# Per-token head attention: the softmax quotient in two vector instructions instead of three

## The chip, the cores and the metric

The kernel runs on one core of a Trainium2 chip. Time is the device time of one execution in microseconds (us); the median of three runs is compared. The core has five engines that run side by side, each strictly in the order of its own queue: TensorE (PE, matrix products; PEld is its weight load), VectorE (DVE), ScalarE (ACT), GpSimd (POOL) and SyncE (SP, which starts transfers). They wait for each other through semaphores. Two memories lie on the core: SBUF[...] and PSUM, into which TensorE writes.

## The reference

The program has two layers: a depthwise convolution with routed experts, and then attention and a second routed network. The change concerns the attention. It is not over tokens but, for every token, over the 16 elements of each of 8 heads:

```python
attn = (q * scale)[..., :, None] * k[..., None, :]   # per token and head: 16 x 16
attn = softmax(attn, axis=-1)
out = einsum('bhlij,bhlj->bhli', attn, v)
```

So for each token, head h and query element i, the result is the sum over j of exp(q_i k_j) v_j, divided by the sum over j of exp(q_i k_j). The tokens are the pixels of 32 images of 56 x 56, 100,352 in all, with 128 channels each.

## The kernel before

The attention stage goes through the tokens in 784 tiles of 128 tokens. Seven tiles are a group, and there are 112 groups. Much of the work is done for two tiles, a pair, at a time, so there are 392 pairs. The steps of a tile or pair, by the function names of the code, with the tile names as the profile writes them:

- keys (TensorE, per pair): keys and values of two tiles into PSUM, kv.
- ends (VectorE, per pair, kx<-kv): the largest and smallest key of every head, two reductions.
- pivots (GpSimd, per pair, kx<-kx, c<-q,kx and c<-c,kx): the key that gives the largest product, c. Three instructions; a pair that crosses a group has one more.
- offsets (VectorE, per tile, s<-kv,c): key minus pivot for 16 x 128 pairs of elements, s.
- scores (GpSimd, per tile, s<-s,q): multiplied by the query, in place.
- exps (ScalarE, per tile, s<-s): the exponential, in place.
- values (VectorE, per tile, ev<-s,kv): exponential times value, ev.
- sums (TensorE, per tile, sm<-ident,s and sm<-ident,ev): the 16 slices of s and of ev are added up in PSUM by transposes that accumulate. The tile sm of a pair holds, for both tiles, the sums of exponentials and the sums of products: [128 channels, 2 tiles, 2 kinds, 128 tokens].
- inverse_first (ScalarE, per pair, r<-sm, r<-r): an approximate inverse r of the sums of exponentials, as exp(-ln(sum)).
- quotients (VectorE, per pair, sm<-sm,r, r<-sm,r and oT<-sm,r): a Newton step for the inverse and the product with it; this is what changes.

Around these lie the head of each group (loading its tokens, normalizing, queries) and its tail (projection, residual, gate logits), mostly on ScalarE and TensorE. A small step of the tail, root_step, has four instructions on GpSimd for every group (st<-st). After every seventh group a pair of images is complete, and choose picks the eight best tokens per expert. It has three long instructions on VectorE: fm<-lg, lg<-fm,lg and pb<-lg,pb, the last a combination of two SBUF tiles.

The order of the work is written out by hand. The wrapper InOrder keeps the order of the text on each of the four compute engines. One loop over k issues, at each turn, work of several tiles: quotients of pair k-6, offsets and scores of tile k, values of tile k-2, and so on; where ends, quotients and pivots go once in two turns, quotients come with an even k, ends and pivots with an odd one. The group_work of places 2k and 2k+1 is the heads, tails and choices; the first of them follows the offsets of its turn on VectorE and precedes the values. So the order on VectorE for a pair of turns is: quotients, offsets, values, ends, offsets, values; on GpSimd: scores, pivots, scores.

All these instructions go through the wrapper, so the profile shows line 161 for each, and they are told apart by their tiles.

Of the kernel before, what the change touches and what calls it, by code (L numbers as in the profile page):

```python
# [8 lines left out]
F32 = mybir.dt.float32  # L9
# [3 lines left out]
ALU = mybir.AluOpType  # L13
# [4 lines left out]
P = 128  # L18
# [7 lines left out]
def conv_attn_hybrid_kernel(  # L26
# [25 lines left out]
    N, C, H, W = x.shape  # L52
# [148 lines left out]
    with tc.tile_pool(name="cv_c", bufs=1) as cc, tc.tile_pool(  # L201
        name="cv", bufs=3
# [147 lines left out]
    with tc.tile_pool(name="rt_c", bufs=1) as cc, tc.tile_pool(  # L350
        name="rt", bufs=4
# [92 lines left out]
    with tc.tile_pool(name="sel", bufs=1) as se, tc.tile_pool(  # L444
        name="sel2", bufs=2
# [257 lines left out]
    with tc.tile_pool(name="sc_c", bufs=1) as cc, tc.tile_pool(  # L703
        name="sc", bufs=4
# [50 lines left out]
        pe, ve, ac = (InOrder(e) for e in (nc.tensor, nc.vector, nc.scalar))  # L755
# [102 lines left out]
    with tc.tile_pool(name="ex_w", bufs=2) as ew, tc.tile_pool(  # L858
        name="ex", bufs=3
# [126 lines left out]
    with tc.tile_pool(name="at_c", bufs=1) as cc, tc.tile_pool(  # L986
        name="at", bufs=2
# [55 lines left out]
        pe, ve, sc, gp = (InOrder(e) for e in (nc.tensor, nc.vector, nc.scalar, nc.gpsimd))  # L1043
# [68 lines left out]
        trs, zrs, roots, qs_, oTs, t2s, us, lgt = ({} for _ in range(8))  # L1112
# [86 lines left out]
        def quotients(n):  # L1199

            r, sm = rs.pop(n), sms.pop(n)
            d = sm[:, :, 0, :]
            ve.tensor_tensor(d, d, r, ALU.mult)
            ve.scalar_tensor_tensor(r, d, -2.0, r, ALU.add, ALU.mult)
            (g, j), (g1, j1) = divmod(n, GJ), divmod(n + 1, GJ)
            for x, y in ((g, j), (g1, j1)):
                if y == 0:
                    oTs[x] = at.tile([C, GJ, P], F32, name="oT")
            if g == g1:
                ve.tensor_tensor(oTs[g][:, j : j + 2, :], sm[:, :, 1, :], r, ALU.mult)  # L1210
            else:
                ve.tensor_tensor(oTs[g][:, j, :], sm[:, 0, 1, :], r[:, 0], ALU.mult)
                ve.tensor_tensor(oTs[g1][:, j1, :], sm[:, 1, 1, :], r[:, 1], ALU.mult)


        def load(g):
# [287 lines left out]
        while k < NT or work or choosing or choices:  # L1504
            tile_work(k, 5, inverse_first, 2)
            tile_work(k, -1, ends, 2)
            tile_work(k, 6, quotients, 2)
            tile_work(k, 0, offsets)
            tile_work(k, -1, pivots, 2)
            tile_work(k, 0, scores)  # L1510
            tile_work(k, -2, keys, 2)
            tile_work(k, 3, sums_ev)
            group_work(2 * k)
            tile_work(k, 1, exps)
            tile_work(k, 2, values)
            tile_work(k, 2, sums_s)
            group_work(2 * k + 1)
            if k == NT + 4:
                for i in range(3):
                    fetch(i)  # L1520
            k += 1
# [3 lines left out]
    with tc.tile_pool(name="f_c", bufs=1) as cc, tc.tile_pool(  # L1525
        name="f", bufs=2
    ) as fp, tc.tile_pool(name="f_p", bufs=1, space=PSUM) as fps, tc.tile_pool(
        name="o", bufs=2
# [114 lines left out]
```

## Time and profile before

| what | us |
|---|---|
| median of three runs | 9744.74 |
| lowest, highest | 9736.06, 9754.17 |
| profiled execution, its own time | 9744.63 |
| profiled execution, span from first to last instruction | 9742.9 |
| attention stage, first offsets to last values | 4733.6 to 9177.5 |
| mean granted TensorE clock, share of full | 0.927 |

| engine | busy us in the span | share |
|---|---|---|
| TensorE (PE) | 8445.6 | 87% |
| VectorE (DVE) | 6563.1 | 67% |
| ScalarE (ACT) | 5231.5 | 54% |
| GpSimd (POOL) | 7059.9 | 72% |

The profile is that of one execution. A row of the groups gives line, engine, operation, the tile written and the tiles read, shapes and count; then the busy time in us and the mean of one instruction in ns; then the time the engine was idle just ahead of these instructions and what ended most of it. A row of the timeline gives the start in us, the duration in us, and the same names. A row of a tile's view gives the count, the shortest, median and longest duration in ns, and the first and last start. A wait that an instruction makes inside its own execution is part of its duration. The shares of the table are means over stages with different limits, so the stage of the change has to be read by itself.

### The profile page before, as it was taken

The numbers are of one execution on the slowest core, as the hardware profiler recorded it, in microseconds if no ns is written. First come the engines' busy times: TensorE is split into PE (matmuls) and PEld (weight loads), VectorE is DVE, ScalarE is ACT, GpSimd is POOL, SyncE is SP. The second block draws the span as 40 slices with busy tenths as digits, with TensorE's granted clock in tenths as the row PEclk, the third lists the DMA queues.
The fourth block names the chain that finished last, engine by engine and source line by source line (L and its number), as shares of the span: only waits on it lengthen the run. The fifth ranks groups of instructions, "written<-read, shape, count | busy, mean of one in ns | idle before, by whom it ended". The sixth has DMA issues, their size and how long they took to land. (4 is left out here: it accounts for less than half of the span.)

```text
span 9742.9 us, 159125 instructions
## 1 busy us (share of the span) xinstructions
PE 8445.6 (87%) x59112; PEld 6817.5 (70%) x59112; DVE 6563.1 (67%) x11135; ACT 5231.5 (54%) x13401; POOL 7059.9 (72%) x5460
## 2 busy tenths in 40 slices
PE   8988255656599999999899999999999999999878
PEld 4446144444367666666689999999999999999833
DVE  3348765556422222222699999999999999999723
ACT  0028422222233333333588888888888888888600
POOL 2228155555578777777899999999999999999600
PEclk9999588888799999999999999999999999999855
DMA  9995055555444444444100100000000000000199
GB/s 180 193 180 173 0 157 148 149 143 150 127 75 61 70 71 69 68 69 68 32 24 31 34 31 31 31 31 31 24 31 34 31 31 31 31 31 24 64 311 333
DMA packets 981784, 828.60 MB, mean 85 GB/s; under 512 B 517844, under 2 KB 873495, under 8 KB 961522
## 3 DMA queue, kind: packets, MB, share of 16 engines
q1 hardware_dynamic: 459410, 473.36, 17.8%
q0 software_dynamic: 177664, 188.81, 11.2%
q10 hardware_dynamic: 343936, 156.26, 6.4%
q8 instruction: 468, 7.67, 0.3%
q14 instruction: 306, 2.51, 0.1%
HBM read 465.46 MB, written 353.64 MB: 84 GB/s over the span
## 5 line engine op out<-in xcount | busy, mean ns | idle before, releaser
L161 POOL TENSOR_TENSOR s<-s,q 128x2048 f32<-128x2048 f32 x784 | 3599.2, 4608 | 74.6 <-DVE s L161 65.9
L161 ACT ACTIVATE s<-s 128x2048 f32<-128x2048 f32 x784 | 1505.0, 1920 | 683.1 <-POOL s L161 680.7
L161 POOL DMA_INDIRECT t_d<-ys,xe x992 | 1530.6, 1543 | 405.7 <-issue 229.0
L161 DVE TENSOR_TENSOR s<-kv,c 128x2048 f32<-128x2048 f32 x784 | 1786.8, 2279 | 20.4 <-POOL c L161 20.4
L161 DVE TENSOR_TENSOR ev<-s,kv 128x2048 f32<-128x2048 f32 x784 | 1784.1, 2276 | 4.5 <-ACT s L161 4.1
L161 PE MATMUL sm<-ident,ev 128*128 128x128 f32 x12544 | 1535.7, 277 | 53.5 <-DVE ev L161 53.5
L161 PE MATMUL sm<-ident,s 128*128 128x128 f32 x12544 | 1512.1, 274 | 8.6 <-ACT s L161 8.5
L161 PEld LDWEIGHTS sm<-ident,ev 128*128 128x128 f32 x12544 | 1438.4, 144 | 104.2 <-DVE ev L161 61.8
L161 PEld LDWEIGHTS sm<-ident,s 128*128 128x128 f32 x12544 | 1391.0, 142 | 21.4 <-ACT s L161 9.4
L932 ACT ACTIVATE hT<-ph,b1t 128x512 f32<-128x512 f32 (+1 forms) x992 | 679.7, 685 | 1236.5 <-PE ph L928 1220.9
L741 POOL DMA_INDIRECT xb_d<-xs,rd x784 | 764.9, 976 | 662.4 <-DVE xs L161 437.2
L943 DVE TENSOR_TENSOR ys<-py,b2t 128x512 f32<-128x512 f32 (+1 forms) x248 | 171.4, 691 | 1541.6 <-PE py L938 1269.3
L938 PEld LDWEIGHTS py<-w,hT 128*128 128x128 f32 x7936 | 958.1, 192 | 201.9 <-issue 91.9
L938 PE MATMUL py<-w,hT 128*128 128x128 f32 x7936 | 982.3, 277 | 0.2
L928 PE MATMUL ph<-xeT,w 128*128 128x512 f32 (+1 forms) x1984 | 921.7, 597 | 69.5 <-DVE xeT L924 69.5
L161 PE MATMUL pa<-rw,ct 128*128 128x256 f32 x1568 | 478.7, 455 | 559.7 <-DVE xs L161 489.4
L161 PEld LDWEIGHTS pa<-rw,ct 128*128 128x128 f32 x1568 | 341.8, 229 | 704.9 <-DVE xs L161 517.4
L161 DVE SCALAR_TENSOR_TENSOR xs<-pa,rst,add 128x256 f32<-128x256 f32 x784 | 351.7, 481 | 544.0 <-remote 432.6
L161 ACT COPY add<-px 128x512 f32<-128x512 f32 x224 | 119.0, 532 | 1043.9 <-remote 671.6
L928 PEld LDWEIGHTS ph<-xeT,w 128*128 128x128 f32 x1984 | 348.6, 191 | 391.8 <-issue 293.3
L240 PE MATMUL cps<-xin,br 56*64 56x448 f32 (+1 forms) x3584 | 452.0, 586 | 52.7 <-ACT ea L273 37.9
L161 PE MATMUL kv<-wq,zT 128*128 128x256 f32 x1568 | 419.4, 391 | 58.6 <-DVE ev L161 58.3
(564 smaller groups left out, 13351.7 us busy)
## 6 DMA issues: line engine op xcount, KB each, us to landing
ct<-conv_d SPq DMA_DIRECT2D x192, 448.0 KB
xin<-in_x_dram SPq DMA_DIRECT2D x128, 392.0 KB
conv_d<-ot ACTq DMA_DIRECT2D x256, 196.0 KB
t_d<-xs ACTq DMA_DIRECT2D x112, 448.0 KB
tr<-t_d SPq DMA_DIRECT2D x112, 448.0 KB
to<-t_d SPq DMA_DIRECT2D x32, 1568.0 KB
out_dram<-oo ACTq DMA_DIRECT2D x32, 1568.0 KB
xg<-in_x_dram SPq DMA_DIRECT2D x96, 448.0 KB
```

What stands on the lines that cost most here:

```text
L161: r = getattr(self.engine, name)(*a, **k)
L240: nc.tensor.matmul(pss[r][b * HP : (b + 1) * HP], bt[rows, w_, :], m_, start=(a == 0), stop=(a == taps - 1), tile_position=(r * HP, b * HP ...
L741: s = nc.gpsimd.indirect_dma_start(out=xb_d, out_offset=bass.IndirectOffsetOnAxis(ap=idx, axis=0), in_=row, in_offset=None, bounds_check=R ...
L928: nc.tensor.matmul(ph[:, :, :rows], w1[:, f * P : (f + 1) * P], xT[:, :, :rows], start=True, stop=True,)
L932: nc.scalar.activation(hT[:, f, :, :rows], ph[:, :, :rows], AF.Gelu, bias=b1t[:, f : f + 1])
L938: nc.tensor.matmul(py[:rows, j, :], hT[:, f, j, :rows], w2[:, f, :], start=(f == 0), stop=(f == NF - 1),)
L943: nc.vector.tensor_tensor(ys[:rows], py[:rows], across(b2t, SB)[:rows], ALU.add)
```

## The change

Before, the Newton step was made on the inverse, and then the inverse was multiplied with the sums of products: with d = sum of exponentials and n = sum of products, d becomes d r in PSUM, r becomes (d - 2) r, and the result is n r. (The sign is taken back in the projection.) Now both sums are first multiplied with the approximate inverse, in one instruction that writes to a new SBUF tile w (two buffers): w holds d r and n r. Then one instruction computes (d r - 2) (n r), which is the same result. Where the two tiles of a pair belong to different groups, this second instruction is issued twice, once per tile.

```diff
             r, sm = rs.pop(n), sms.pop(n)
-            d = sm[:, :, 0, :]
-            ve.tensor_tensor(d, d, r, ALU.mult)
-            ve.scalar_tensor_tensor(r, d, -2.0, r, ALU.add, ALU.mult)
+            w = at.tile([C, 2, 2, P], F32, name="w", bufs=2)
+            ve.tensor_tensor(w, sm, r.unsqueeze(2).to_broadcast([C, 2, 2, P]), ALU.mult)
             (g, j), (g1, j1) = divmod(n, GJ), divmod(n + 1, GJ)
...
             if g == g1:
-                ve.tensor_tensor(oTs[g][:, j : j + 2, :], sm[:, :, 1, :], r, ALU.mult)
+                parts = [(oTs[g][:, j : j + 2, :], slice(0, 2))]
             else:
-                ve.tensor_tensor(oTs[g][:, j, :], sm[:, 0, 1, :], r[:, 0], ALU.mult)
-                ve.tensor_tensor(oTs[g1][:, j1, :], sm[:, 1, 1, :], r[:, 1], ALU.mult)
+                parts = [(oTs[g][:, j : j + 1, :], slice(0, 1)), (oTs[g1][:, j1 : j1 + 1, :], slice(1, 2))]
+            for to, i in parts:
+                ve.scalar_tensor_tensor(
+                    to, w[:, i, 0, :], -2.0, w[:, i, 1, :], ALU.add, ALU.mult
+                )
```

## The prediction

> **What bounds the kernel now.** I read the windows first, to see which engine is full in the attention stage. It holds all of the change: its first quotient starts at 4762.2 us and its last at 9186.7, 391 gaps, (9186.7 - 4762.2) / 391 = 11.32 us per pair of tiles.
>
> ```profile
> core 0: us, PE busy (x) PEld busy (x) DVE busy (x) ACT busy (x) POOL busy (x), PEclk, DMA share, GB/s
> 5500.00:9200.00 3700.00, 3577.81 (x29802) 3382.27 (x29799) 3619.36 (x3182) 3074.85 (x7693) 3525.90 (x2043) 0.99 0.09 32
> ```
>
> VectorE (DVE) is busy for 97.8% of the stage and GpSimd (POOL) for 95.3%. Two in-order engines are nearly full at once, and each feeds the other. The groups of the same window say with what:
>
> ```profile
> L161 POOL TENSOR_TENSOR s<-s,q 128x2048 f32<-128x2048 f32 x648 | 2975.5, 4609 | 64.2 <-DVE s L161 56.7 <-DVE fsm L161 6.5
> L161 DVE TENSOR_TENSOR ev<-s,kv 128x2048 f32<-128x2048 f32 x650 | 1479.2, 2276 | 4.4 <-ACT s L161 4.1
> L161 DVE TENSOR_TENSOR s<-kv,c 128x2048 f32<-128x2048 f32 x647 | 1474.5, 2279 | 6.7 <-POOL c L161 6.7
> ...
> L161 DVE SCALAR_TENSOR_TENSOR r<-sm,r 128x256 f32<-128x256 f32 x326 | 138.3, 424 | 11.2
> L161 DVE TENSOR_TENSOR sm<-sm,r 128x256 f32<-128x256 f32 x326 | 138.2, 424 | 5.6 <-ACT r L161 5.6
> ```
>
> GpSimd multiplies scores (4.6 us a tile) out of two SBUF tiles, s and q. Every VectorE instruction that works on each tile or pair has at most one input in SBUF: kv and sm lie in PSUM. Last, the timeline of each of the two (start, duration) shows where the quotients stand against the scores:
>
> ```profile
> 7108.06 0.62 POOL L161 TENSOR_TENSOR c<-q,kx 128x256 f32<-128x256 f32 x1
> 7108.76 0.62 POOL L161 TENSOR_TENSOR c<-c,kx 128x256 f32<-128x256 f32 x1
> 7109.34 4.58 POOL L161 TENSOR_TENSOR s<-s,q 128x2048 f32<-128x2048 f32 x1
> ```
>
> ```profile
> 7107.22 2.27 DVE L161 TENSOR_TENSOR ev<-s,kv 128x2048 f32<-128x2048 f32 x1
> 7109.42 0.42 DVE L161 TENSOR_TENSOR sm<-sm,r 128x256 f32<-128x256 f32 x1
> 7109.87 0.42 DVE L161 SCALAR_TENSOR_TENSOR r<-sm,r 128x256 f32<-128x256 f32 x1
> 7110.33 0.42 DVE L161 TENSOR_TENSOR oT<-sm,r 128x256 f32<-128x256 f32 x1
> 7110.68 2.28 DVE L161 TENSOR_TENSOR s<-kv,c 128x2048 f32<-128x2048 f32 x1
> ```
>
> The quotients fall at the start of a scores instruction, and the next offsets (s<-kv,c) are queued behind them. VectorE's steps, start to start, are 2.20 for each offsets or values, 0.66 for the two reductions and 1.26 for the quotients: 4 x 2.20 + 0.66 + 1.26 = 10.72 us, the gap of an undisturbed pair. GpSimd's are 2 x 4.56 + 1.57 = 10.69.
>
> **The change, by instructions.** Removed: three VectorE instructions (1.26 us with the step to the next). Added: one multiply 128x512 out of PSUM and SBUF. The nearest row has just this form, a PSUM operand and a broadcast SBUF operand:
>
> ```profile
> L1575 DVE TENSOR_TENSOR fhT<-p_ft,hb 128x512 f32<-128x512 f32 x16 | 11.1, 692 | 39.6 <-PE p_ft L1573 39.6
> ```
>
> So 0.69, with 0.03 to a dependent instruction 0.72. Then one Newton step 128x256, 0.42, of which 0.34 counts to the next independent start. Together 1.06: **0.20 us less per pair**, 78 us over 391, if nothing waits. Pairs that cross a group (one in seven) have two Newton steps of 128x128, some 0.25 more, against two small products before. PSUM sm comes free earlier, which nothing waits for. DMAs do not change.
>
> **The change, by ports.** The Newton step now reads w twice, so both its inputs are in SBUF, while GpSimd's scores read SBUF as well. The trace has this meeting elsewhere. First VectorE begins, then GpSimd:
>
> ```profile
> 7077.22 3.42 DVE L161 SCALAR_TENSOR_TENSOR pb<-lg,pb 128x3136 f32<-128x3136 f32 x1
> ```
>
> ```profile
> 7077.47 7.56 POOL L161 TENSOR_TENSOR s<-s,q 128x2048 f32<-128x2048 f32 x1 [1.10 <-DVE s L161]
> ```
>
> Scores take 7.56 there instead of 4.57: GpSimd does nothing until VectorE's two-SBUF instruction is through. The other order occurs once, in the routing stage:
>
> ```profile
> 1162.44 2.24 POOL L568 TENSOR_TENSOR kept<-kept,eq 128x784 f32<-128x784 f32 x1
> ```
>
> ```profile
> 1163.53 1.97 DVE L567 SCALAR_TENSOR_TENSOR eq<-rk,eq 128x784 f32<-128x784 f32 x1
> ...
> 1168.56 0.97 DVE L567 SCALAR_TENSOR_TENSOR eq<-rk,eq 128x784 f32<-128x784 f32 x1
> ```
>
> Here the VectorE instruction takes 1.97 instead of 0.97. It ends at 1165.50, which is 0.82 after GpSimd's end (1162.44 + 2.24 = 1164.68): it began about 0.15 before that end. The trace thus shows a wait of 1.0 us, not one of 4. The Trainium skill ("SBUF — State Buffer", section "Who interferes with whom") goes further: whichever of a two-SBUF-input VectorE instruction and a GpSimd instruction that reads SBUF comes first holds the shared read interface for the whole instruction, and the other is fully blocked. By the longest wait that the row shows, 1.0 us, the change costs (1.0 - 0.2) x 391 = 313 us; by the rule the wait runs to the end of scores. I take the rule, since both rows fit it to the end of the holder and neither shows a time limit.
>
> **How long it waits.** Time 0 is the start of the scores of an even tile. In the timeline scores start some 0.15 after their offsets end where they wait for them (offsets 7075.02 to 7077.30, scores 7077.47). VectorE: values -0.23, reductions 1.97, offsets of the odd tile 2.63, values 4.83, the multiply 7.03, the Newton step issued at 7.75. GpSimd: scores 0 to 4.54, the three pivot instructions to 6.11, the odd tile's scores 6.11 to 10.68. The Newton step finds them running and can begin about 0.14 before their end: a wait of **2.8 us**. It ends at 10.96, the offsets run 10.88 to 13.16, and the next scores start at 13.31. So the cycle is **13.31 us**, with GpSimd idle for 2.6 us because what it needs is queued behind the instruction that waits for it. The cycle holds itself: to escape, the Newton step would have to be issued before 6.11, 1.6 us earlier, and GpSimd's only other work (four small inverse-root instructions, 1.06 us per seven tiles) is shorter. The multiply, the exponentials on ScalarE and TensorE's sums are all ready earlier; keys too.
>
> Extras per pair: crossing pairs (0.14 of pivots and 0.25) / 7 = 0.06. The inverse roots, 1.06 every 3.5 pairs, lie on GpSimd's path for half of the groups: 0.15 (0 to 0.30). The choice of tokens puts three 3.4 us instructions on VectorE every 24.5 pairs, between an offsets and a values. At an odd tile the slack takes most of the two plain ones (0.5 each), at an even tile they cost 2.3 each; pb's own hold of the port costs 3.0 to 3.4. Mean 6.0 per choice, 0.25 per pair (now 10 us per choice, which is part of the 11.34 below). Sum 13.31 + 0.06 + 0.15 + 0.25 = 13.77.
>
> The first 30 pairs (4762.2 to 5092.3, 11.0 us a gap) are different: there GpSimd lags, and the Newton step would meet the short pivot instructions, 0.4 us before their end. Whether it or the next scores then gets the port no row shows: 0 to +75 us, I take 30. From 5092.3 on: 361 gaps of (9186.7 - 5092.3) / 361 = 11.34 now, 13.77 then: 361 x 2.43 = 877. The profiled execution's own time is 9744.6 (span 9742.9), equal to the median of 9744.7. 9744.6 + 877 + 30 = 10,652, rounded to **10,650 us**.
>
> **Rivals.**
> 1. *The lock holds only part of the time* (12%). If delays let GpSimd lag again, as in the first 30 pairs, about half of the pairs escape: +450, 10,190. Against it: a pair without a wait needs that lag, and each wait removes it.
> 2. *No wait: faster* (6%). If the two reads share the port, or so short an instruction slips in between GpSimd's elements, VectorE saves 0.20 x 391: 9667. It decides at one price: as soon as the mean wait exceeds 0.20 us per pair the sign turns. For it: no row has a 256-element case. Against it: the row with 1.97.
> 3. *GpSimd pays* (5%). If VectorE always goes first, scores grow by about 0.28 (the Newton step less its 0.14 of overlap): GpSimd needs 10.69 + 0.30 + 0.28 = 11.27 against 11.32 now, and VectorE has 0.20 less: 9720 to 9760, no change. That speaks from the row with 7.56, but there VectorE was first by 0.25 us.
>
> **How the numbers follow.** The lock throughout has 77%. Its own range: 13.43 (half of the choices, no other extra) to 13.92 (all roots on the path), that is 361 x 2.09 = +755 to 361 x 2.58 + 75 = +1006: 10,500 to 10,750, about nine in ten of its chance; outside it a slightly different arbitration. To hold eight in ten the range takes in the upper part of rival 1 and some more above: 10,330 to 10,850. Slower by over 0.2% (20 us, about what a measurement of this kernel can tell from no change): 77 + 12 + 1 = 90%. Faster: 6 + 1 = 7%. Same: 3%.
>
> **What would show it.** The Newton step, oT<-w, has a mean near 3 us instead of 0.42, with most of it wait; w<-sm,r has 0.69. Scores on GpSimd keep 4.6, but their idle time "<-DVE s" grows from 57 us to 2 to 3 us a pair, some 900 us. VectorE still looks almost full, since its wait is counted as busy; GpSimd falls to near 80%. Gaps between quotients stand at 13.3 instead of 10.7. Stages before 4731 us and after 9200 keep their times. The prediction is wrong if oT<-w stays near 0.42 (rival 2), if scores grow instead (rival 3), or if long runs of pairs keep 10.5 to 11 (rival 1).

## The result and the profile after

The changed kernel takes 10,588.9 us (median of 5 runs, 10,585.4 to 10,596.4) against 9742.0 us before (also five runs, the three of the table above among them): a ratio of 1.087, 95% interval 1.0856 to 1.0885. It is 847 us slower; 10,650 was forecast. The profiled execution has a span of 10,585.8 us, 842.9 more than before. From the first offsets to the end of the last values the attention stage took 4733.6 to 9179.7 us before, 4446 us; it takes 4725.7 to 10,018.1 now, 5292 us. So the whole difference, 846 us, lies in this stage.

The windows of the changed kernel, for the same stretch as before:

```profile
core 0: us, PE busy (x) PEld busy (x) DVE busy (x) ACT busy (x) POOL busy (x), PEclk, DMA share, GB/s
5500.00:9200.00 3700.00, 3152.00 (x24724) 2912.24 (x24725) 3690.32 (x2378) 2582.05 (x6402) 2944.51 (x1698) 0.96 0.07 25
```

VectorE is busy for 99.7% and GpSimd for 79.6%, down from 95.3%. The higher share of VectorE is no work: the groups of the attention stage show where it comes from.

```profile
L161 POOL TENSOR_TENSOR s<-s,q 128x2048 f32<-128x2048 f32 x784 | 3597.2, 4590 | 900.8 <-DVE s L161 479.2 <-ACT sq L161 135.3 <-ACT lg L161 76.9
...
L161 DVE SCALAR_TENSOR_TENSOR oT<-w 128x256 f32<-128x256 f32 x448 | 1145.5, 2567 | 13.5
...
L161 DVE TENSOR_TENSOR w<-sm,r 128x512 f32<-128x512 f32 x392 | 264.9, 676 | 4.9 <-ACT r L161 4.9
```

The multiply w<-sm,r costs what was worked out for it (0.68 us), the scores as much as before (4.59). The mean of oT<-w, 2567 ns, mixes two shapes. The view by form keeps them apart; it begins here with the 31st pair:

```profile
L161 DVE SCALAR_TENSOR_TENSOR oT<-w 128x256 f32<-128x256 f32 x309 | 927.4, 3001 | 10.6
...
L161 DVE SCALAR_TENSOR_TENSOR oT<-w 128x128 f32<-128x128 f32 x104 | 197.3, 1936 | 1.8
```

The Newton step of a whole pair takes 3.00 us where 0.42 was the price of its kind. The second row has the half steps of pairs that cross a group. GpSimd is idle for 901 us ahead of its scores, up from 75. The names in that idle time are inferred, and not all of them are the cause: ScalarE's sq and lg had no part in the input of the scores. The timelines of one locked pair, first VectorE, then GpSimd (start, duration):

```profile
7516.58 2.27 DVE L161 TENSOR_TENSOR s<-kv,c 128x2048 f32<-128x2048 f32 x1
7518.77 2.27 DVE L161 TENSOR_TENSOR ev<-s,kv 128x2048 f32<-128x2048 f32 x1
7520.97 0.68 DVE L161 TENSOR_TENSOR w<-sm,r 128x512 f32<-128x512 f32 x1
7521.68 3.07 DVE L161 SCALAR_TENSOR_TENSOR oT<-w 128x256 f32<-128x256 f32 x1
7524.67 2.28 DVE L161 TENSOR_TENSOR s<-kv,c 128x2048 f32<-128x2048 f32 x1
```

```profile
7513.81 4.56 POOL L161 TENSOR_TENSOR s<-s,q 128x2048 f32<-128x2048 f32 x1 [2.69 <-DVE s L161]
7518.32 0.23 POOL L161 TENSOR_TENSOR kx<-kx 128x16 f32<-128x16 f32 x1
7518.62 0.62 POOL L161 TENSOR_TENSOR c<-q,kx 128x256 f32<-128x256 f32 x1
7519.32 0.62 POOL L161 TENSOR_TENSOR c<-c,kx 128x256 f32<-128x256 f32 x1
7519.90 4.56 POOL L161 TENSOR_TENSOR s<-s,q 128x2048 f32<-128x2048 f32 x1
7527.09 4.55 POOL L161 TENSOR_TENSOR s<-s,q 128x2048 f32<-128x2048 f32 x1 [2.63 <-DVE s L161]
```

This is the cycle of the prediction. The Newton step is issued at 7521.68, 1.8 us after the odd tile's scores have begun. It ends at 7524.75, 0.29 us after the scores end (7519.90 + 4.56 = 7524.46). Only then come the offsets, and 0.14 us after these the next scores, which had nothing else to wait for: GpSimd stood still for 2.63 us. From scores to scores of the next even tile it is 7527.09 - 7513.81 = 13.28 us.

### The profile page after: what moved, and what is told of

It reads as the page before. It is cut to its first block, busy times and chain, and to the rows that moved or that the text cites. A ratio compares the mean times of both kernels' runs of the same rounds, so it can differ in the third digit from the quotient of the medians.

```text
span 10585.8 us, 158740 instructions
## 1 busy us (share of the span) xinstructions
PE 8702.5 (82%) x59112; PEld 6955.1 (66%) x59112; DVE 7464.8 (71%) x10743; ACT 5263.1 (50%) x13401; POOL 7069.9 (67%) x5460
## 3 DMA queue, kind: packets, MB, share of 16 engines
q1 hardware_dynamic: 459410, 473.36, 16.3%
## 5 line engine op out<-in xcount | busy, mean ns | idle before, releaser
L161 POOL TENSOR_TENSOR s<-s,q 128x2048 f32<-128x2048 f32 x784 | 3597.2, 4590 | 900.8 <-DVE s L161 479.2
L161 PE MATMUL sm<-ident,ev 128*128 128x128 f32 x12544 | 1654.6, 289 | 588.1 <-DVE ev L161 587.6
L161 PEld LDWEIGHTS sm<-ident,ev 128*128 128x128 f32 x12544 | 1515.2, 150 | 710.4 <-DVE ev L161 667.2
L161 DVE SCALAR_TENSOR_TENSOR oT<-w 128x256 f32<-128x256 f32 x448 | 1145.5, 2567 | 13.5
```

The lines of the kernel that those rows point to most:

```text
L161: r = getattr(self.engine, name)(*a, **k)
```

## The experiments

The theory: VectorE reads from both memories (kv and sm lie in PSUM), but the Newton step's two SBUF inputs make it wait for the end of a GpSimd instruction that reads SBUF, and the price is large since the offsets for GpSimd's next scores are queued behind it. The rivals: the step is slow by itself (it reads a tile just written), or VectorE's waiting costs the same wherever it lies. The experiments ran on other chips of the kind; each is compared with runs of the kernel before on its own chip (9321.9, 9324.4 and 9744.1 us). The changed kernel as it stands was not run there; its 847 us are from the first chip. The 420 us between chips lie ahead of the attention: in the second millisecond the granted TensorE clock was 0.77 in the profile of before and 0.91 in that of the first experiment, from a faster chip. In the attention the mean gap of a pair is the same in these two profiles (11.32 and 11.31 us). Absolute times in the expectations are on the first chip's scale, with 9742 for before.

### One SBUF input

The place and the form of the Newton step stay; only its first operand remains in PSUM.

```diff
-            w = at.tile([C, 2, 2, P], F32, name="w", bufs=2)
-            ve.tensor_tensor(w, sm, r.unsqueeze(2).to_broadcast([C, 2, 2, P]), ALU.mult)
+            d = sm[:, :, 0, :]
+            w = at.tile([C, 2, P], F32, name="w", bufs=2)
+            ve.tensor_tensor(d, d, r, ALU.mult)
+            ve.tensor_tensor(w, sm[:, :, 1, :], r, ALU.mult)
...
-                    to, w[:, i, 0, :], -2.0, w[:, i, 1, :], ALU.add, ALU.mult
+                    to, d[:, i, :], -2.0, w[:, i, :], ALU.add, ALU.mult
```

> The Newton step keeps its new place as last instruction, but its first operand (sums of exponentials times inverse) stays in PSUM and only the products lie in the SBUF tile w, so it reads one SBUF tile; the multiply is two instructions of 128x256. Port theory: the Newton step oT falls from a mean of 2.6 us to 0.42, gaps of a pair return to 10.7 to 11.6, time 9690 to 9750 (three instructions with one dependence less: 0.34 + 0.45 + 0.34 = 1.13 us instead of 1.26). Rival, that the Newton step is slow by itself because it reads a tile just written: oT stays near 3 us and the time near 10590.

Measured: 9325.1 us, ratio 1.0003 (0.9993 to 1.0012). The view of the tile oT (shortest, median, longest in ns):

```profile
L161 DVE SCALAR_TENSOR_TENSOR oT<-sm,w x448: 280/424/427, 4339.9 to 8763.1; 128x256 f32<-128x256 f32 x112, 128x128 f32<-128x128 f32 x38
```

No instance is longer than 427 ns, while it still reads a tile written just before, and although 316 of the 448 began when the scores of that moment had over 0.5 us to run. The whole loss is gone with one of the two SBUF operands, and with it the rival that the step is slow by itself. The small gain that I expected of one dependence less did not come: the two multiplies start 0.47 us apart, as if the second depended on the first.

### The holder cut in two

GpSimd's scores of an odd tile, which the Newton step waits for, are two instructions of half the length:

```diff
-            gp.tensor_tensor(
-                s3, s3, qs_[g][:, 1, j].unsqueeze(1).to_broadcast([P, HD, C]), ALU.mult
-            )
+            m = 2 if n % 2 else 1
+            for i in range(m):
+                h = slice(i * HD // m, (i + 1) * HD // m)
+                gp.tensor_tensor(
+                    s3[:, h], s3[:, h],
+                    qs_[g][:, 1, j].unsqueeze(1).to_broadcast([P, HD // m, C]), ALU.mult,
+                )
```

> The changed kernel, but GpSimd's scores of every odd tile are two instructions of 128x1024. Port theory: the Newton step waits to the end of the half that runs when it is issued (halves 6.1 to 8.4 and 8.4 to 10.8 in the locked cycle, issued at 7.75), so 0.5 us instead of 2.8; oT has a mean of 0.8 to 1.2 us, the cycle falls from 13.3 to 11.1 to 11.5, time 9740 to 9850 (one more GpSimd instruction and one hold of 0.3 us a pair). Rival, slow by itself: oT stays near 3 us, time 10590 to 10640.

Measured: 9611.0 us, ratio 1.0314 (1.0297 to 1.0331), +289 us. The view of oT:

```profile
L161 DVE SCALAR_TENSOR_TENSOR oT<-w x448: 278/1050/2461, 4332.8 to 9042.0; 128x256 f32<-128x256 f32 x112, 128x128 f32<-128x128 f32 x38
```

The Newton step falls to a mean of 1.30 us (0.8 to 1.2 was expected), and pairs without a crossing or a choice of tokens have gaps of 11.25 us on average instead of 13.05 in the changed kernel (10.90 in the kernel before). The wait follows the length of the GpSimd instruction, as the theory has it. But the total is far above the +0 to +110 expected. The pairs that cross a group issue two Newton steps. After the first, GpSimd begins its second half before the second Newton step is there, and this one waits again (one at 7149.78 takes 2.00 us, its twin 2.45). Such pairs are 14.3 us long (11.2 before): about 56 x 3.1 = 171 of the 289.

### Behind the offsets

The Newton step is issued as a function of its own (newton, which takes w from a dictionary), behind offsets of the same turn. Only the line that calls it is shown:

```diff
...
             tile_work(k, 0, offsets)
+            tile_work(k, 6, newton, 2)
```

> The changed kernel, but the Newton step is issued behind the next offsets instead of ahead of them. Theory that the loss is GpSimd's idle time, because its next scores need offsets that are queued behind the waiting instruction: the Newton step still waits, but the next scores can follow at once, GpSimd's idle time falls from 2.6 us a pair to 0.3, time 9700 to 9850. Rival, that VectorE's own waiting is the price wherever it lies: time stays within 200 of 10590. If the next scores got the port before the waiting Newton step, its wait would grow by 4.6 us a pair: above 11000; the first 30 pairs of the changed kernel speak against that.

Measured: 9592.4 us, ratio 1.0293 (1.0276 to 1.031), +271 us, outside the expected +0 to +110. Yet pairs without a crossing or a choice of tokens have a gap of 10.94 us against 10.90 before, though the Newton steps of a whole pair have a mean of 0.89 us, 0.47 of it wait, and GpSimd's idle time ahead of its scores falls from 901 to 120 us. The 10590 of the rival is far off; why 0.47 us of wait cost these pairs so little is taken up below, with the versions side by side. Nearly all of the loss lies in crossing pairs, 16.35 us each against 11.22. The timelines show why, VectorE first:

```profile
4624.20 1.78 DVE L161 SCALAR_TENSOR_TENSOR oT<-w 128x128 f32<-128x128 f32 x1
```

```profile
4625.91 4.62 DVE L161 SCALAR_TENSOR_TENSOR oT<-w 128x128 f32<-128x128 f32 x1
```

```profile
4625.80 4.58 POOL L161 TENSOR_TENSOR s<-s,q 128x2048 f32<-128x2048 f32 x1
```

The first of the two waits for the scores in progress. The next scores, whose offsets are ready in this order, then start at 4625.80, 0.11 us ahead of the second Newton step, which waits for the whole of them. The values behind it are late, and so is all that follows.

### The same without a second step

Crossing pairs take the three instructions of the kernel before, all others stay behind the offsets. Parts of the difference from the version before:

```diff
-            w = at.tile([C, 2, 2, P], F32, name="w", bufs=2)
-            ve.tensor_tensor(w, sm, r.unsqueeze(2).to_broadcast([C, 2, 2, P]), ALU.mult)
-            ws[n] = w
...
             if g == g1:
...
+                w = at.tile([C, 2, 2, P], F32, name="w", bufs=2)
+                ve.tensor_tensor(w, sm, r.unsqueeze(2).to_broadcast([C, 2, 2, P]), ALU.mult)
+                ws[n] = w
+                return
+            d = sm[:, :, 0, :]
+            ve.tensor_tensor(d, d, r, ALU.mult)
+            ve.scalar_tensor_tensor(r, d, -2.0, r, ALU.add, ALU.mult)
+            ve.tensor_tensor(oTs[g][:, j, :], sm[:, 0, 1, :], r[:, 0], ALU.mult)
+            ve.tensor_tensor(oTs[g1][:, j1, :], sm[:, 1, 1, :], r[:, 1], ALU.mult)
...
```

> The Newton step behind the next offsets, as tried, but pairs that cross a group (56 of 392) take the three instructions of the kernel before. In the last trials such pairs were 16.4 us long, since GpSimd's next scores started between their two Newton steps and the second waited for all of them. If this was the whole loss of that version, its +270 us falls by 50 x 5.2 = 260: time within 30 us of the kernel before (ratio 0.998 to 1.004). If the remaining pairs lose too: ratio above 1.01.

Measured: 9402.0 us, ratio 1.0082 (1.0067 to 1.0098), +78 us. The long pairs are gone, 10.8 instead of 16.3 us from values to values, and with them 193 of the 271 us. The rest was not expected:

```profile
L161 DVE SCALAR_TENSOR_TENSOR oT<-w x336: 406/874/2770, 4344.5 to 8844.0; 128x256 f32<-128x256 f32 x168
```

The one Newton step of the other 336 pairs has a mean of 1.06 us, 0.64 of it wait, 214 us in all. In the version before it was 0.47; I take it that the long pair had changed how the two engines stood to each other, but no run settles that.

### Behind the odd tile's offsets, where the pivots are

```diff
...
             tile_work(k, 0, offsets)
+            tile_work(k, 7, newton, 2)
```

> The changed kernel, but the Newton step is issued one turn later, behind the offsets of the odd tile, where GpSimd stands in its three short pivot instructions (4.5 to 6.1 us of the locked cycle, Newton step issued at 4.8). Port theory: it waits at most one pivot instruction, 0.6 us; oT has a mean of 0.5 to 1.0 us, time 9680 to 9800. Rival, slow by itself: oT near 3 us, time near 10590.

Measured: 9374.6 us, ratio 1.0061 (1.0044 to 1.0078), +53 us, at the upper end of the expectation. Same instructions as the changed kernel, one turn later, and 794 us of its 847 are back. The view of oT:

```profile
L161 DVE SCALAR_TENSOR_TENSOR oT<-w x448: 281/814/4634, 4340.1 to 8807.7; 128x256 f32<-128x256 f32 x112, 128x128 f32<-128x128 f32 x38
```

The mean is 0.90 us. The time came as expected, but not for the reason given: once the lock is gone the two engines drift against each other, 337 of the 448 Newton steps still began while scores ran, and the longest takes 4.63 us, far more than a step behind one pivot instruction would. What is gone is the lock. Most of the 53 us lies in the crossing pairs again (12.06 us against 11.22); the plain ones have 10.95 against 10.90.

The versions side by side, from their traces: plain pairs, those without a crossing or a choice of tokens, from the 31st on, in us per pair (the version without a second step from values to values, the others from quotients to quotients).

| version | gap | wait in the Newton step | idle time of VectorE | the rest: VectorE's own work |
|---|---|---|---|---|
| the kernel before | 10.92 | 0 | 0.18 | 10.74 |
| the changed kernel | 13.29 | 2.71 | 0.03 | 10.55 |
| scores of odd tiles halved | 11.29 | 0.70 | 0.04 | 10.55 |
| behind the even offsets | 10.96 | 0.49 | 0.00 | 10.47 |
| the same without a second step | 11.15 | 0.68 | 0.00 | 10.46 |
| behind the odd offsets | 10.96 | 0.49 | 0.00 | 10.47 |

With a wait, VectorE is full in every version, and the gap is its own work plus the wait. So a microsecond of wait costs a microsecond wherever the Newton step stands; some 0.45 us of it are paid for by the shorter work and by the 0.18 us that VectorE was idle before. The rival is right on the price and wrong on the amount: what is queued behind the Newton step decides how long it waits. In the changed kernel GpSimd cannot go on without the offsets behind it, so each Newton step meets the scores in their first half, as in the locked pair above; with the offsets ahead of it GpSimd goes on, and the mean wait is 0.5 to 0.7 us.

### Without the long holder

In both kernels GpSimd multiplies only the first of the 16 slices of the scores by the query; the other 15 are left out.

```diff
-                s3, s3, qs_[g][:, 1, j].unsqueeze(1).to_broadcast([P, HD, C]), ALU.mult
+                s3[:, :1], s3[:, :1], qs_[g][:, 1, j].unsqueeze(1).to_broadcast([P, 1, C]), ALU.mult
```

> The kernel before with GpSimd's scores cut to the first of 16 slices (the multiplication of the other 15 by the query is left out). VectorE alone is then full. Port theory: GpSimd held nothing up before, so little is gained: gaps of undisturbed pairs stay at 10.7, time 0 to 80 us under the kernel before.

> The changed kernel with the same cut of the scores. Port theory: with the long holder gone the Newton step runs in 0.42 to 0.6 us, gaps of undisturbed pairs are 10.5, and the change gives its own saving of 0.20 us x 391 = 78 us against the cut kernel before (60 to 90), where the full kernel lost 847. Rival, slow by itself: it stays 700 us or more behind the cut kernel before.

Measured: the cut kernel before 9263.9 us (ratio to the full one 0.9936, 0.9921 to 0.9951), 60 us less than the full one and within the expectation; the cut changed kernel 9231.4 us (0.990, 0.9884 to 0.9915). The change now gains 33 us (four runs each; the slowest of the one, 9238.5, is below the fastest of the other, 9254.8). The view of oT in the cut changed kernel:

```profile
L161 DVE SCALAR_TENSOR_TENSOR oT<-w x448: 281/425/428, 4330.4 to 8664.4; 128x256 f32<-128x256 f32 x112, 128x128 f32<-128x128 f32 x38
```

Not one of 448 waits. So what makes the change slow is its meeting with GpSimd's long instruction, not its own instructions. The saving is half of what was expected. The instructions give all of it: from the first of them to the next offsets it is 7014.37 - 7013.31 = 1.06 us in the timeline of the cut changed kernel, and 7014.71 - 7013.45 = 1.26 in that of the cut kernel before (at a crossing 1.13 and 1.33). But VectorE's reductions wait longer for TensorE's keys. The waits (us in total, times, longest) of the cut kernel before, then of the cut changed kernel:

```profile
DVE kx L161 <- PE kv L161: 5.6, 19, 0.7
```

```profile
DVE kx L161 <- PE kv L161: 41.7, 60, 1.4
```

So 36 of the 392 x 0.20 = 78 us went over into waiting for TensorE, which is busy for 98% of the stage in the one (97% in the other).

### The single multiply without a second SBUF input

No two-SBUF read, and the single multiply kept: it writes in place into PSUM, ScalarE copies the products to SBUF, and the Newton step reads one operand from each, behind the values of the tile. Parts of the difference from the changed kernel:

```diff
-            r, sm = rs.pop(n), sms.pop(n)
-            w = at.tile([C, 2, 2, P], F32, name="w", bufs=2)
-            ve.tensor_tensor(w, sm, r.unsqueeze(2).to_broadcast([C, 2, 2, P]), ALU.mult)
+            sm = sms[n]
+            ve.tensor_tensor(
+                sm, sm, rs.pop(n).unsqueeze(2).to_broadcast([C, 2, 2, P]), ALU.mult
+            )
+
+        def products(n):
+
+            w = ws[n] = at.tile([C, 2, P], F32, name="w", bufs=2)
+            sc.copy(w, sms[n][:, :, 1, :])
+
+        def newton(n):
+
+            w, sm = ws.pop(n), sms.pop(n)
...
-                    to, w[:, i, 0, :], -2.0, w[:, i, 1, :], ALU.add, ALU.mult
+                    to, sm[:, i, 0, :], -2.0, w[:, i, :], ALU.add, ALU.mult
...
             tile_work(k, 6, quotients, 2)
+            tile_work(k, 6, products, 2)
...
             tile_work(k, 2, values)
+            tile_work(k, 6, newton, 2)
```

> A version without any two-SBUF read: one multiply of 128x512 in place in PSUM, the products copied to SBUF by ScalarE, the Newton step from PSUM and SBUF behind the values of the tile. VectorE has 0.20 us less per pair as the change meant, ScalarE some 0.45 more (it is busy for 83% of the stage). If VectorE sets the pace: ratio 0.992 to 0.997. If ScalarE's copy comes late or sm, held 5 us longer, delays TensorE's sums: no gain or some loss, ratio 1.00 to 1.03.

Measured: 9308.2 us (11 runs) against 9324.4 (15 runs), ratio 0.9983 (0.9974 to 0.9992): 16 us less than the kernel before, clear of noise, but under what was expected and inside the 0.2% that was called no change. Its groups:

```profile
L161 DVE TENSOR_REDUCE kx<-kv 128x16 f32<-128x256 f32 x784 | 292.6, 414 | 88.7 <-PE kv L161 88.4
...
L161 DVE SCALAR_TENSOR_TENSOR oT<-sm,w 128x256 f32<-128x256 f32 x448 | 166.3, 381 | 4.2 <-ACT w L161 4.2
```

The Newton step hardly waits (4 us in all), but the reductions wait 88 us for keys, 44 more than in the profile of the kernel before. The last run asked whether the longer use of sm was to blame. It is the same kernel with newton behind offsets instead of values:

```diff
             tile_work(k, 0, offsets)
+            tile_work(k, 6, newton, 2)
...
             tile_work(k, 2, values)
-            tile_work(k, 6, newton, 2)
```

> The version with ScalarE's copy, its Newton step behind the offsets instead of the values of the tile, so that sm comes free 2.2 us sooner. In the version behind the values the two reductions waited 88 us for TensorE's keys. If held sm was the cause, that wait falls below 50 us and the ratio to 0.994 to 0.997. If ScalarE's copy then comes too late, oT waits for w (4 us in all so far) by more than 40 us and the ratio rises to 1.000 or more.

```profile
L161 DVE TENSOR_REDUCE kx<-kv 128x16 f32<-128x256 f32 x784 | 295.1, 420 | 46.2 <-PE kv L161 46.2
...
L161 DVE SCALAR_TENSOR_TENSOR oT<-sm,w 128x256 f32<-128x256 f32 x448 | 168.9, 388 | 102.9 <-ACT w L161 101.2
```

Measured: 9752.8 against 9744.1 us, ratio 1.001 (1.0001 to 1.0019). Both halves of the expectation came true at once: the wait for keys is back at 46 us (45 in the kernel before), so the longer use of sm was to blame, and in exchange the Newton step waits 101 us for ScalarE's copy. Moving it between the two places only changes the engine that is waited for.

## Why the prediction was right

- *The wait.* Right: it runs to the end of the scores, as the rule that the prediction took has it; the one row of the trace before, with its 1.0 us, could not tell that. In the locked pair above the Newton step takes 3.07 us where it needs 0.42: 2.65 against the 2.8 forecast. Two conditions of it are shown by experiment: with one SBUF operand less no instance waits, and with GpSimd's long instruction cut none does either.
- *What is queued behind.* Right, and shown: with the offsets of the even tile ahead of it, the wait of a plain pair falls from 2.7 to 0.5 us and its gap from 13.3 to 11.0; behind the offsets of the odd tile all but 53 us come back. The queue sets the length of the wait, not its price.
- *The cycle and its lock.* 13.31 was worked out, 13.28 is what the pair above shows, and the median gap of a pair is 13.43. After the first choice of tokens no gap is below 12.96 us, but for the last two of the stage: nothing escaped.
- *The extras.* From the 31st pair on the mean gap is 13.67 where 13.77 was summed: 36 us too many over 361 gaps. One term was too large: 0.25 us for the second, half-wide Newton step of a crossing pair, where the cut changed kernel shows 1.13 - 1.06 = 0.07. That is 0.03 a pair, 9 of the 36; the rest was not taken apart.
- *The first 30 pairs.* An open point of the forecast, 30 us taken of 0 to 75; they cost 5. Timelines of VectorE and of GpSimd in that stretch:

```profile
4889.04 0.75 DVE L161 SCALAR_TENSOR_TENSOR oT<-w 128x256 f32<-128x256 f32 x1
```

```profile
4888.89 0.62 POOL L161 TENSOR_TENSOR c<-c,kx 128x256 f32<-128x256 f32 x1
4889.47 4.77 POOL L161 TENSOR_TENSOR s<-s,q 128x2048 f32<-128x2048 f32 x1
```

  The Newton step waits for the pivot instruction to end at 4889.51 and then goes ahead of the scores that follow, which take 4.77 instead of about 4.57. These two terms, 36 and 25, are the difference between 10,650 and 10,589.
- *The saving.* The 0.20 us per pair was right as a price. That it would be worth 78 us without a wait was not: it was 33 us without the long holder, where the keys became the next thing to wait for, and 16 us in the version with ScalarE's copy. In the full kernel there is one more limit, which the prediction worked out and did not set against its 78 us: GpSimd's own 10.69 us a pair lie only 0.03 below VectorE's 10.72. So the 9667 of rival 2 was too low; how much too low, no run shows by itself.
- *The other rivals.* GpSimd did not pay: its scores have 4590 ns against 4608. Nor did the lock hold only part of the time, once the first choice of tokens had set it.

## What to carry to other kernels

Count, for each instruction that is merged or moved, how many of its operands come from SBUF, and look at what GpSimd does at that time: here one more SBUF operand turned a saving of 0.2 us into a wait of 2.6. The wait was long in every pair because what the other engine needed next was queued behind it, so look at the queue, not only at the two instructions that meet. And set a saving on one engine against the next one that is nearly full: in this stage three engines were over 95% busy, and a saving of 78 us on one of them brought 33 us or less.

## What the runs showed of the hardware beyond that

- A Newton step that waited at the port was served ahead of GpSimd's next instruction, even when that one had its inputs: in the version behind the even offsets, of the 351 Newton steps that began while scores ran and waited, none saw a second GpSimd instruction end before it. One that comes 0.11 us after GpSimd's next one has started gets no such turn and waits for all of it, 4.62 us.
- The wait ends some 0.14 us before the end of the GpSimd instruction as the profile records it. In the changed kernel 374 of the 448 Newton steps waited, 351 for scores and 23 for a pivot instruction; without its own 0.42 or 0.28 us, the median of them ends 0.138 us before the one GpSimd instruction that ended meanwhile, and nine in ten lie between 0.131 and 0.141. The row of the routing stage has about 0.15.
